# A recurrent layer's weights moved into tiles of their own, and all its loads moved to one queue

## The chip, the core and the metric

The kernel runs on one core of one Trainium2 chip. A core has a matrix engine (TensorE, "PE" in the profile), a vector engine (VectorE, "DVE"), an engine for functions and scaled copies (ScalarE, "ACT"), a general engine (GpSimd, "POOL") and an engine that mostly issues transfers (SyncE, "SP"). Each works through an instruction queue of its own, in order. SyncE and ScalarE issue the transfers (DMAs) here. Data lie in SBUF (128 partitions), results of matmuls in PSUM, inputs and outputs in the chip's main memory. The metric is the time of one execution on the device, in microseconds (us).

## The reference, cut to what matters

Four layers are applied one after the other to x (32 sequences of 64 tokens with 256 features), with a second input y of the same shape (ctx_2048 below).

```python
x = L0(x, y, ...)    # cross attention over channels, batches of 64 x 256
x = L1(x, y, ...)    # self attention, cross attention to y, MLP 256 -> 1024 -> 256
x = L2(x, y, ...)    # the same with other weights
x = L3(x, y, ...)    # recurrent layer, with state from y
```

The recurrent layer, L3, shortened:

```python
xn = _ln(x, ln1_w, ln1_b)
sx = _token_shift(xn, state[:, i1])
xxx = jnp.tanh((xn + sx * maa_x) @ maa_w1).reshape(b, l, 5, 1, EXTRA_MAA)
xxx = jnp.matmul(xxx, maa_w2).reshape(b, l, 5, E)
x5 = xn[:, :, None] + sx[:, :, None] * (maa_stack + xxx)
w = jnp.exp(-jnp.exp(time_decay + jnp.tanh(x5[:, :, 1] @ decay_w1) @ decay_w2))
r, k, v = x5[:, :, 3] @ Wr.T, x5[:, :, 0] @ Wk.T, x5[:, :, 2] @ Wv.T   # split in 32 heads of 8
g = silu(x5[:, :, 4] @ Wg.T)
# for each token: out = r (u * k v + s);  s = k v + w * s
att = group_norm(outs) * gn_w + gn_b
x = x + att * g @ Wo.T
xn2 = _ln(x, ln2_w, ln2_b); sx2 = _token_shift(xn2, state[:, i0])
xk, xr = xn2 + sx2 * ffn_maa_k, xn2 + sx2 * ffn_maa_r
x = x + sigmoid(xr @ ffn_Wr.T) * (square(relu(xk @ ffn_Wk.T)) @ ffn_Wv.T)
```

## The kernel before

The 2048 tokens are four groups (g = 0 to 3) of 512, and x stays in SBUF throughout. Layers 0, 1 and 2 go by groups, the MLPs by half groups of 256 tokens, the recurrent layer by eight slabs of 256 tokens (half a group each).

*Order.* Every layer is cut into pieces, small functions that emit a few instructions. `timed` spreads the pieces over a stretch of a made-up time axis, `emit` sorts all pieces by that time and runs them. On this axis layer 0 lies between -7.0 and -0.2 (L0_AT), the weights of layer 1's self attention at -4.0 (L0_LOAD), the MLP weights of layer 1 at 0.8 (MLP_LOAD), the self attention of L1 from 0 to 4, its cross attention from 4 to 8, and so on. The times are no times of the chip: they give each instruction a rank, and the tile framework then orders the queue of each engine by rank among the instructions which are ready by its own reckoning, so that a piece of a late rank with nothing to wait for can come early. It also adds the waits between engines. The transfers' completions are counted in eight counters in turn; a transfer waits for the one that was issued eight places before it, on whichever queue.

*Space.* Tiles come from pools. `const`, `small`, `psum`, `dram` and `work` are open all the time. `lw` and `lp` hold what the attention layers need, and are closed when these have been emitted. Then a pool `r` opens for the recurrent layer in the same place; with `reuse_waits="tile"` each of its tiles waits for the last users of the tiles of `lw` and `lp` that lay at its address, and all its instructions come behind the last instruction of these two pools in the order. The tag `big` in `work` is a ring of three buffers of 8 KB per partition, which the raw weights, the contexts ctxT, the MLP's hidden halves (hT) and the recurrent layer's products (vb) use in turn.

*The attention and MLP weights.* `staged` (L946) loads raw weights into `big` from SyncE, and ScalarE and VectorE split them into a high and a low part (`split_weights`, L956, L957; `split`, L178, L179; L1034, L1035).

*The recurrent pool* (L1081 to L1142). Eighteen tiles are loaded here: the W tiles (256 KB each) from SyncE, the small ones from ScalarE's queue, in the order of the code; `hold` only reserves places, so that each tile comes to lie where it does:

```python
def load(name, shape, src, eng=nc.scalar):
    c3[name] = pool.tile(shape, FP, name=name, bufs=1)
    eng.dma_start(c3[name], src)
```

*A slab* (`recurrent`). Its first part is: `norm` (statistics L146 to L152, x normalized on ScalarE at L155 into xn_r; TensorE transposes it, L163, and multiplies it with the matrix `step`, L170; ScalarE evacuates both, L625 and L632; GpSimd sets the first tokens from `st01`, L636), `first_mix` (L652), `maa` (products with mw1, L192 and L666, tanh at L671, a small rearranging transfer tb, L674), five times `mix` (product with mw2a or mw2b, L682, L686, L689), and the projections `vals` (Wv), `recept` (Wr), `keys` (Wk), `decay_a` and `decay_b` (dw1, dw2), `own_term` (selu, made from sel at L1137), `gate` (Wg). Its second part brings v through main memory into vb (`spread`, L722), multiplies it with k (L780), runs the scan (L795) and reads it with r (L780, pa at L808); norm, gate and Wo follow (L831, L841). Its third part is the feed-forward step (ffn_Wk, ffn_Wr, ffn_Wv) and the output (L884).

*Where the layers meet.* The last six half groups of L2's MLP (`late`: names L2m with pf, hf, hT, pfo) are put into the recurrent layer's plan, so that TensorE has work beside the slabs. L2's cross attention (names L2c) ends just before; its last output projection is po_L2c with the weights wo.

Of the kernel before, what the change touches and what calls it, by code (L numbers as in the profile page):

```python
# [15 lines left out]
FP = mybir.dt.float32  # L16
# [5 lines left out]
B, S, E = 32, 64, 256  # L22
T = B * S
P = 128
# [7 lines left out]
XM = 32  # L32
# [30 lines left out]
W3 = {n: i for i, n in enumerate(["Wk", "Wv", "Wr", "Wg", "Wo", "ffn_Wk", "ffn_Wr", "ffn_Wv"])}  # L63


def timed(pieces, t0, t1):

    total, at, out = sum(c for c, _ in pieces) or 1.0, 0.0, []
    for c, piece in pieces:
        out.append((t0 + (t1 - t0) * (at + c / 2) / total, piece))  # L70
        at += c
    return out


def emit(*timed_lists):
    for _, piece in sorted((p for ps in timed_lists for p in ps), key=lambda p: p[0]):
        piece()
# [3 lines left out]
def tile_xattn_stack(ctx: ExitStack, tc: tile.TileContext, a: dict, out: bass.AP):  # L81
    nc = tc.nc
    PSUM = bass.MemoryType.PSUM

    const = ctx.enter_context(tc.tile_pool(name="const", bufs=1))
# [31 lines left out]
    def row(name):  # L117

        r = const.tile([P, E], FP, tag="row", name=name, bufs=3)
        nc.scalar.dma_start(r, a["rows"][ROW[name]].partition_broadcast(P))  # L120
        return r
# [770 lines left out]
        return first, second, third  # L892


    wts = {}

    with tc.tile_pool(name="lw", bufs=1) as wp, tc.tile_pool(name="lp", bufs=2) as pool:
        m1 = wp.tile([P, S], FP, name="m1")
# [41 lines left out]
        def staged(name, k, parts):  # L940

            n = sum(n for _, n in parts)
            raw = work.tile([P, k, n], FP, tag="big", name=f"raw_{name}", bufs=3)
            at = 0
            for key, m in parts:
                nc.sync.dma_start(raw[:, :, at : at + m], a[key].rearrange("(c p) n -> p c n", p=P))  # L946
                at += m
            return raw

        def split_weights(w, raw, cols, scale=None, to=None):  # L950

            to = to or cols
            for c in range(raw.shape[1]):
                src, hi, lo = raw[:, c, cols], w[:, 0, c, to], w[:, 1, c, to]
                if scale:
                    nc.scalar.activation(hi, src, AF.Identity, bias=tiny[:, 2:3], scale=vec(scale, c))  # L956
                    nc.vector.scalar_tensor_tensor(lo, src, vec(scale, c), hi, ALU.mult, ALU.subtract)  # L957
                else:
                    split(hi, lo, src)
# [61 lines left out]
        def load_mlp(L):  # L1021
            def go():
                wts[L, "b2"] = row(f"{L}_b2")
                b = small.tile([P, 8], FP, tag="b1", name=f"b1_{L}", bufs=2)
                raw = staged(f"w1_{L}", 2, [(f"{L}_w1", FF)])
                ps = through(f"w1_{L}", raw, f"{L}_ln3_b", 8)
                nc.vector.tensor_tensor(b, vecs[:, VEC[f"{L}_b1"] : VEC[f"{L}_b1"] + 8], ps[:, :8], ALU.add)
                w1 = work.tile([P, 2, 2, FF], FPR, tag="w1", name=f"w1_{L}", bufs=1)
                split_weights(w1, raw, slice(0, FF), f"{L}_ln3_s")
                raw = staged(f"w2_{L}", 8, [(f"{L}_w2", E)])  # L1030
                w2 = work.tile([P, 2, 8, E], FPR, tag="w2", name=f"w2_{L}", bufs=1)
                for i in range(2):
                    cs = slice(4 * i, 4 * i + 4)
                    nc.scalar.copy(w2[:, 0, cs], raw[:, cs])  # L1034
                    nc.vector.tensor_tensor(w2[:, 1, cs], raw[:, cs], w2[:, 0, cs], ALU.subtract)  # L1035
                wts[L, "m"] = {"w1": w1, "w2": w2, "b1": b}
            return go
# [11 lines left out]
        plan = [timed(layer0(pool), *L0_AT), loads(load_self("L1"), L0_LOAD, L0_LOAD + 2.0)]  # L1049
        late = []  # L1050
        for i, L in enumerate(("L1", "L2")):
            for k in range(2):
                for g in range(NG):
                    a_ = (3 * i + k, f"{L}{'sc'[k]}", g, pool)
                    if k:
                        proj, core = attention(*a_, ctx_of(g), lambda L=L: wts[L, 2], mask_cross(g))
                    else:
                        proj, core = attention(*a_, None, lambda L=L: wts[L, 1], mask_self)
                    at = (8 + GAP) * i + 4 * k + g
                    p0 = at + PROJ + (CPROJ if k else 0)  # L1060
                    if g == 0 and (i or k):
                        plan.append(loads((load_cross if k else load_self)(L), p0 - 0.9, p0 - 0.001))
                    plan += [timed(proj, p0, p0 + PROJ_D), timed(core, at, at + CORE_D)]
            at = (8 + GAP) * i + MLP
            for g in range(NG):
                for u in range(2):
                    p = mlp_half(3 * i + 2, f"{L}m{g}{u}", g, u, lambda L=L: wts[L, "m"], lambda L=L: wts[L, "b2"])
                    if i and g:

                        s = (2 * g + u - 2) * SLOT + M2  # L1070
                        late += timed(p, s, s + M2_D)
                        continue
                    plan.append(timed(p, at, at + MLP_D))
                    at += MLP_S
            load = at - MLP_S + MLP_D + 0.001 if i == 0 else None
            plan.append([(load, load_mlp("L2"))] if i == 0 else [(MLP_LOAD, load_mlp("L1"))])
        emit(*plan)

    with tc.tile_pool(name="r", bufs=2, reuse_waits="tile") as pool:  # L1081
        c3 = {}

        def load(name, shape, src, eng=nc.scalar):
            c3[name] = pool.tile(shape, FP, name=name, bufs=1)
            eng.dma_start(c3[name], src)

        def load_w(*names):
            for n in names:
                load(n, [P, 2, E], a["w3"][W3[n]].rearrange("(c p) n -> p c n", p=P), nc.sync)  # L1090

        def hold(tag, bufs=2, shape=None):
            pool.tile(shape or [P, 2, RR], FP, tag=tag, name=f"hold_{tag}", bufs=bufs)

        def shifted_ring(name):

            c3[name] = ring(pool, name, [P, 2, RB, S], 2, lambda t: nc.gpsimd.memset(t[:, :, :, 0], 0.0))

        load("mw1", [P, 2, 5 * XM], a["maa_w1"].rearrange("(c p) n -> p c n", p=P))
        load("mw2a", [P, E], a["maa_w2"][:P])  # L1100
        load("mw2b", [XM, E], a["maa_w2"][P:])
        load("step", [P, P], a["step"])
        load("st01", [P, 2, B, 2], a["st01"])
        load("dw1", [P, 2, 64], a["decay_w1"].rearrange("(c p) n -> p c n", p=P))
        hold("fx")
        hold("dfx")
        load("avg", [P, P], a["avg"])
        hold("x5", 3)
        hold("nx", 1)
        shifted_ring("wsh")  # L1110
        hold("xk")
        hold("xr")
        hold("kk")
        hold("x")
        hold("rr", 2, [P, 2, E])
        hold("dx")
        load_w("Wv", "Wr", "Wk")
        shifted_ring("vsh")

        load("sel", [P, 2, P], a["sel"])  # L1120
        load("dw2", [64, E], a["decay_w2"])
        hold("ta", 1, [P, RR + S])
        hold("vT")
        hold("rT")
        hold("tb", 1, [XM, RR])
        hold("rk", 1)
        hold("dT", 1, [64, RR])
        selu = c3["selu"] = pool.tile([P, 2, P], FP, name="selu", bufs=1)
        load_w("Wg", "Wo", "ffn_Wk", "ffn_Wr", "ffn_Wv")
        load("s0", [P, 2, RS, B], a["s0"])  # L1130
        hold("gt")
        hold("at")
        hold("sq", 1)
        shifted_ring("ksh")
        hold("nfx", 1)
        for c in range(2):
            nc.vector.tensor_scalar(selu[:, c], c3["sel"][:, c], vec("L3_faaaa", c), None, ALU.mult)  # L1137
        gnh = c3["gnh"] = pool.tile([P, 4], FP, name="gnh", bufs=1)
        for i, n in enumerate(("L3_gn_w", "L3_gn_b")):
            nc.vector.tensor_scalar(  # L1140
                gnh[:, 2 * i : 2 * i + 2], vecs[:, VEC[n] : VEC[n] + 2], 0.5, None, ALU.mult
            )  # L1142
        r = [recurrent(n, pool, c3) for n in range(2 * NG)]
        plan = []
        for n, (first, second, third) in enumerate(r):
            at = n * SLOT + START
            plan += [timed(first[:1], at - LEAD, at - LEAD), timed(first[1:], at, at + R1_D)]
            at += R2
            plan += [timed(second, at, at + R2_D)]
            at += R2_D + F0  # L1150
            plan += [timed(third[:1], at, at), timed(third[1:], at + F1, at + F1 + F1_D)]
        plan.append(late)
        emit(*plan)
# [78 lines left out]
```

## Time and profile before

| | before |
|---|---|
| median of 3 runs | 1092.89 us (1092.37 to 1093.71) |
| profiled execution | 1097.71 us |
| its span | 1095.9 us |
| mean granted TensorE clock | 0.958 |
| TensorE busy | 985.5 us |
| VectorE busy | 813.4 us |
| ScalarE busy | 551.0 us |
| GpSimd busy | 532.2 us |
| share of 16 DMA engines: SyncE's queue (q1) | 16.5%, 48.55 MB |
| share of 16 DMA engines: ScalarE's queue (q10) | 1.2%, 3.16 MB |

The stages of the profiled execution: layer 0 and the first loads up to about 104 us, layers 1 and 2 to about 706 us, recurrent layer with the last MLP halves to the end.

How to read it. The profile is of one execution; the medians are of others, without a profile. Busy time of TensorE is the modelled time of its matmuls. A group "out<-in" names the tile that is written and those that are read. "SPq" and "ACTq" are the issues of transfers from SyncE's and ScalarE's queues; their duration is that of the issue and not of the transfer. A wait "A <- B: 5.8, 1, 5.8" says that A waited 5.8 us in all for B, once, 5.8 us at most. The chain of waits goes back from the last instruction to what released it each time, so that its pieces add up to the span.

### The profile page before, as it was taken

To read this page: it belongs to the slowest core of one execution; us is meant where nothing else is said; L and a number is where in the kernel's file an instruction comes from. 1 tells how busy PE (TensorE), PEld (TensorE's weight loads), DVE (VectorE), ACT (ScalarE), POOL (GpSimd) and SP (SyncE) were. 2 spreads that over 40 slices of the span, in tenths; PEclk is the share of its full clock that TensorE was granted. 3 is DMA by queue.
4 is the path that set the end of the run, shared out by engine and by line. 5 is a ranking of instruction groups with operands and counts; after the bars stand their busy time and mean duration, and the time that the engine had idled before them with its cause. 6 is when DMAs were issued, how large, how long until landed. Compare 5 with 4: busy or idle time off the path is not lost.

```text
span 1095.9 us, 26331 instructions
## 1 busy us (share of the span) xinstructions
PE 985.5 (90%) x10764; PEld 789.9 (72%) x10764; DVE 813.4 (74%) x1513; ACT 551.0 (50%) x1271; POOL 532.2 (49%) x552
## 2 busy tenths in 40 slices
PE   8998999899989999989989999898889989869757
PEld 5777776667778989867767778786767777647535
DVE  5754687878877545687778777549798897988873
ACT  5643653555555645754555454354446554345234
POOL 4243766767756435566557756342534523233300
PEclk9899998999999999988999999999999999989788
DMA  9100111111100000141011101222222122430300
GB/s 300 42 21 20 20 47 31 39 24 26 29 16 20 27 1 21 50 130 41 21 41 27 26 22 31 59 79 50 61 66 50 41 59 56 121 87 21 87 10 29
DMA packets 45947, 53.39 MB, mean 49 GB/s; under 512 B 16146, under 2 KB 40068, under 8 KB 43780
## 3 DMA queue, kind: packets, MB, share of 16 engines
q1 hardware_dynamic: 38756, 48.55, 16.5%
q10 hardware_dynamic: 7072, 3.16, 1.2%
q8 instruction: 85, 1.39, 0.5%
q14 instruction: 34, 0.28, 0.1%
HBM read 38.83 MB, written 4.21 MB: 39 GB/s over the span
## 4 chain that ended last, share of the span: by engine, by line
PE 41%; DVE 35%; POOL 8%; ACT 7%; DMA 4%; issue 4%; SPq 1%; ACTq 0%; POOLq 0%; DVEq 0%
DVE vb_r L795 6%; DVE vb_r L780 4%; PE pf_L1m L187 4%; PE pfo_L1m L187 3%; POOL s_L2c L463 2%; PE pfo_L2m L187 2%; DVE x L198 2%; PE pr L312 2%; POOL s_L1c L463 2%; PE pf_L2m L187 2%; DVE x_r L686 1%; PE pq_L2c L187 1%; PE px_r L682 1%; DVE s_L1c L458 1%; POOL s_L1s L463 1%
## 5 line engine op out<-in xcount | busy, mean ns | idle before, releaser
L689 POOL TENSOR_TENSOR x_r<-x_r,xn_r 128x512 f32<-128x512 f32 x40 | 58.2, 1463 | 93.2 <-DVE x_r L686 91.0
L795 DVE TENSOR_TENSOR_SCAN vb_r<-wsh,vb_r 128x512 f32<-128x512 f32 x64 | 76.4, 1250 | 5.9 <-ACT wsh L693 5.9
L187 PE MATMUL pf_L2m<-lnT_L2m,w_L 128*128 128x256 f32 x384 | 57.0, 302 | 6.5 <-DVE lnT_L2m L179 3.7
L463 POOL TENSOR_TENSOR s_L1s<-s_L1s,n 128x512 f32<-128x512 f32 x32 | 43.1, 1358 | 39.8 <-DVE s_L1s L458 39.1
L187 PEld LDWEIGHTS pf_L2m<-lnT_L2m,w_L 128*128 128x128 f32 x384 | 51.1, 200 | 10.7 <-DVE lnT_L2m L179 4.3
L187 PE MATMUL pfo_L2m<-w_L,hT_L2m 128*128 128x256 f32 x384 | 55.4, 293 | 1.6 <-DVE hT_L2m L581 1.5
L463 POOL TENSOR_TENSOR s_L2s<-s_L2s,n 128x512 f32<-128x512 f32 x32 | 43.1, 1365 | 27.0 <-DVE s_L2s L458 26.3
L187 PE MATMUL pfo_L1m<-w_L,hT_L1m 128*128 128x256 f32 x384 | 54.5, 288 | 1.6 <-POOL hT_L1m L580 0.8
L463 POOL TENSOR_TENSOR s_L2c<-s_L2c,n_L2c 128x512 f32<-128x512 f32 x32 | 41.7, 1322 | 29.2 <-DVE s_L2c L458 28.2
L187 PE MATMUL pf_L1m<-lnT_L1m,w_L 128*128 128x256 f32 x384 | 52.0, 288 | 3.9 <-ACT hf_L1m L577 1.2
L463 POOL TENSOR_TENSOR s_L1c<-s_L1c,n_L1c 128x512 f32<-128x512 f32 x32 | 41.3, 1308 | 24.3 <-DVE s_L1c L458 23.2
L187 PEld LDWEIGHTS pf_L1m<-lnT_L1m,w_L 128*128 128x128 f32 x384 | 47.5, 191 | 7.2 <-ACT hf_L1m L577 2.1
L187 PEld LDWEIGHTS pfo_L2m<-w_L,hT_L2m 128*128 128x128 f32 x384 | 49.3, 192 | 4.8 <-DVE hT_L2m L581 1.9
L187 PEld LDWEIGHTS pfo_L1m<-w_L,hT_L1m 128*128 128x128 f32 x384 | 49.2, 191 | 3.5 <-POOL hT_L1m L580 1.0
L580 POOL TENSOR_SCALAR hT_L1m<-hf_L1m 128x512 fp32r<-128x512 f32 x32 | 21.9, 684 | 55.4 <-ACT hf_L1m L577 53.5
L132 PE MATMUL pa_r<-vb_r,sel 128*32 128x256 f32 x256 | 23.2, 494 | 27.7 <-DVE vb_r L780 25.3
L577 ACT ACTIVATE hf_L1m<-pf_L1m,b_L 128x256 f32<-128x256 f32 x64 | 26.7, 472 | 42.3 <-PE pf_L1m L187 39.7
L581 DVE TENSOR_TENSOR hT_L1m<-hf_L1m,hT_L1m 128x512 fp32r<-128x512 f32 x32 | 25.3, 791 | 30.2 <-POOL hT_L1m L580 30.1
L580 POOL TENSOR_SCALAR hT_L2m<-hf_L2m 128x512 fp32r<-128x512 f32 x32 | 26.7, 840 | 42.7 <-ACT hf_L2m L577 42.6
L577 ACT ACTIVATE hf_L2m<-pf_L2m,b_L 128x256 f32<-128x256 f32 x64 | 26.6, 472 | 36.4 <-PE pf_L2m L187 29.4
L780 DVE TENSOR_TENSOR vb_r<-vb_r,ksh 128x2048 f32<-128x2048 f32 x16 | 40.1, 2523 | 4.4 <-DMA vb_r<-vd_r 4.4
L282 ACT ACTIVATE att<-pe,nmx 128x256 f32<-128x256 f32 x64 | 29.6, 478 | 20.2 <-DVE nmx L280 17.6
(388 smaller groups left out, 3073.3 us busy)
## 6 DMA issues: line engine op xcount, KB each, us to landing
vb_r<-vd_r SPq DMA_DIRECT2D x16, 1024.0 KB, 7.1
raw_w_L<-in_L_w_dram SPq DMA_DIRECT2D x4, 1024.0 KB, 12.4
y<-in_y_dram SPq DMA_DIRECT2D x8, 256.0 KB, 5.3
x<-in_x_dram SPq DMA_DIRECT2D x8, 256.0 KB, 4.8
ctxT_L1c<-in_yT_dram SPq DMA_DIRECT2D x4, 512.0 KB, 3.7
kbd<-kT_L1s SPq DMA_DIRECT2D x64, 32.0 KB, 2.0
kbd<-kT_L1c SPq DMA_DIRECT2D x64, 32.0 KB, 2.0
kbd<-kT_L2s SPq DMA_DIRECT2D x64, 32.0 KB, 2.2
```

Of the source, the lines that this page charges most:

```text
L132: return lambda: nc.tensor.matmul(ps, sta, mov, start=start, stop=stop)
L187: nc.tensor.matmul(ps, sta[x], mov[y], start=(at == 0), stop=(at == n - 1))
L198: nc.vector.tensor_tensor(xs, xs, ps, ALU.add)
L282: nc.scalar.activation(att[:, 2 * h + c, :], pe[:, c, :], AF.Exp, bias=nmx[:, h, c : c + 1], accum_out=rs[:, h, c : c + 1],)
L312: nc.tensor.matmul(pr[:, m, h, :], att[:, 2 * h + c, m * P : (m + 1) * P], xvT[:, c, h, :], start=(c == 0), stop=(c == 1),)
L463: nc.gpsimd.tensor_tensor(s[:, r], s[:, r], n(j).unsqueeze(1).broadcast_to([P, 8, S]), ALU.add)
L577: nc.scalar.activation(raw[:, i], ps[:, i], AF.Gelu_apprx_tanh, bias=w()["b1"][:, 2 * f2 + i : 2 * f2 + i + 1])
L580: nc.gpsimd.tensor_scalar(h[:, 0], raw, 1.0, 0.0, ALU.mult, ALU.add)
L581: nc.vector.tensor_tensor(h[:, 1], raw, h[:, 0], ALU.subtract)
L689: nc.gpsimd.tensor_tensor(d, d, st["x"], ALU.add)
L780: nc.vector.tensor_tensor(v, v, x.unsqueeze(1).broadcast_to([P, 4, 2 * RR]), ALU.mult)
L795: nc.vector.tensor_tensor_scan(v[:, d], flat(st["wsh"]), v[:, d], 0.0, ALU.mult, ALU.add)
```

## The change

A function `load_early` is put into the plan of the attention layers, at 4.0, the start of layer 1's cross attention. It loads twelve tiles (step, mw1, st01, mw2a, mw2b, Wv, Wr, Wk, dw1, dw2, sel, avg) from SyncE's queue into the pool `const`, where they have places of their own to the end. The remaining six loads of the recurrent pool (Wg, Wo, ffn_Wk, ffn_Wr, ffn_Wv, s0) stay where they were in the program and all go to SyncE's queue; s0 was on ScalarE's. So the recurrent pool holds less, and its tiles move to lower addresses. To make room, the framework's scratch for software-issued DMAs is given 1024 bytes per partition; in the kernel before it had 16,384.

```diff
-    wts = {}
+    wts, c3 = {}, {}
+
+    def load_to(pool, name, shape, src):
+        c3[name] = pool.tile(shape, FP, name=name, bufs=1)
+        nc.sync.dma_start(c3[name], src)
+
+    def load_early():
+
+        load_to(const, "step", [P, P], a["step"])
+        load_to(const, "mw1", [P, 2, 5 * XM], a["maa_w1"].rearrange("(c p) n -> p c n", p=P))
+        load_to(const, "st01", [P, 2, B, 2], a["st01"])
+        load_to(const, "mw2a", [P, E], a["maa_w2"][:P])
+        load_to(const, "mw2b", [XM, E], a["maa_w2"][P:])
+        for n in ("Wv", "Wr", "Wk"):
+            load_to(const, n, [P, 2, E], a["w3"][W3[n]].rearrange("(c p) n -> p c n", p=P))
+        load_to(const, "dw1", [P, 2, 64], a["decay_w1"].rearrange("(c p) n -> p c n", p=P))
+        load_to(const, "dw2", [64, E], a["decay_w2"])
+
+        load_to(const, "sel", [P, 2, P], a["sel"])
+        load_to(const, "avg", [P, P], a["avg"])
...
+        plan.append([(4.0, load_early)])
         emit(*plan)
...
-        c3 = {}
-
-        def load(name, shape, src, eng=nc.scalar):
-            c3[name] = pool.tile(shape, FP, name=name, bufs=1)
-            eng.dma_start(c3[name], src)
+        def load(name, shape, src):
+            load_to(pool, name, shape, src)
 
         def load_w(*names):
             for n in names:
-                load(n, [P, 2, E], a["w3"][W3[n]].rearrange("(c p) n -> p c n", p=P), nc.sync)
+                load(n, [P, 2, E], a["w3"][W3[n]].rearrange("(c p) n -> p c n", p=P))
...
-        load("mw1", ...), load("mw2a", ...), load("mw2b", ...), load("step", ...), load("st01", ...), load("dw1", ...)
         hold("fx")
         hold("dfx")
-        load("avg", [P, P], a["avg"])
...
-        load_w("Wv", "Wr", "Wk")
         shifted_ring("vsh")
-
-        load("sel", [P, 2, P], a["sel"])
-        load("dw2", [64, E], a["decay_w2"])
...
-    nc = bacc.Bacc("TRN2", target_bir_lowering=False, num_devices=1)
+    nc = bacc.Bacc("TRN2", target_bir_lowering=False, num_devices=1, dynamic_dma_scratch_size=1024)
```

## The prediction

> **What bounds the kernel now.** I read the page first, then the chain of waits in order of time, then the waits of the stretch where the chain rests on DMAs, then the busy time by window around it.
>
> ```profile
> PE 985.5 (90%) x10764; PEld 789.9 (72%) x10764; DVE 813.4 (74%) x1513; ACT 551.0 (50%) x1271; POOL 532.2 (49%) x552
> ...
> PE 41%; DVE 35%; POOL 8%; ACT 7%; DMA 4%; issue 4%; SPq 1%; ACTq 0%; POOLq 0%; DVEq 0%
> ```
>
> TensorE is busy for 90% of the span, and 41% of the chain that ended last is TensorE, 35% VectorE; DMA is 4%. Loading weights is therefore nothing in general and can only matter in a few places. The largest of them lies where the attention layers end and the recurrent layer begins:
>
> ```profile
> 704.12 1.64 PE pf_L2m L187 x12
> ...
> 705.78 0.84 ACT hf_L2m L577 x2
> ...
> 706.73 2.32 DMA mw2b<-in_maa_w_dram
> ...
> 709.07 3.35 DMA avg<-in_avg_dram
> ...
> 712.45 0.61 ACT xn_r L155
> ...
> 713.10 0.33 PE pln_r L163
> ```
>
> For 2.32 + 3.35 = 5.67 us the chain consists of loads (mw2b, avg), with a matmul before and the recurrent layer's first normalization (xn_r, L155) after. The waits of 703 to 732 us, and the windows, say who pays:
>
> ```profile
> DVE selu L1137 <- DMA sel<-in_sel_dram: 6.3, 1, 6.3
> ACT xn_r L155 <- DMA avg<-in_avg_dram: 5.8, 1, 5.8
> ```
>
> ```profile
> 706.00:708.00 2.00, 1.54 (x13) 1.34 (x13) 1.75 (x4) 0.62 (x2) 0.62 (x1) 1.00 0.53 148
> 708.00:710.00 2.00, 2.00 (x19) 2.00 (x18) 0.06 (x1) 0.00 (x0) 0.00 (x0) 1.00 0.63 128
> 710.00:712.00 2.00, 0.52 (x5) 0.32 (x3) 0.00 (x0) 0.00 (x0) 0.00 (x0) 1.00 1.10 337
> 712.00:714.00 2.00, 0.90 (x7) 0.77 (x8) 0.00 (x0) 1.55 (x4) 0.00 (x0) 1.00 0.91 307
> 714.00:716.00 2.00, 2.00 (x14) 2.00 (x13) 1.64 (x3) 2.00 (x6) 1.26 (x2) 0.64 0.39 129
> 716.00:718.00 2.00, 2.00 (x12) 2.00 (x11) 1.70 (x4) 2.00 (x5) 0.22 (x1) 0.51 0.00 0
> 718.00:720.00 2.00, 2.00 (x18) 1.61 (x17) 0.73 (x2) 1.50 (x4) 1.04 (x2) 1.00 0.03 8
> ```
>
> (Columns: busy PE, PEld, DVE, ACT, POOL, then the granted clock, DMA share, GB/s.) ScalarE stands still for 5.83 us because ten load issues lie in its queue in front of xn_r, and in the compiled program a DMA waits for the one issued eight places before it, so the later ones wait for the earlier ones to land. The MLP's GELUs (L577) queue behind them, so TensorE runs out too: 0.46 us idle in 706 to 708, 1.48 in 710 to 712, 1.10 in 712 to 714, 3.04 in all. Then it works at a granted clock of about 0.5 until 718.
>
> **The change, part by part.**
>
> *Ten loads leave ScalarE's queue.* Nine go to SyncE's early loads, s0 to SyncE's late ones. Their issue rows in the timeline are 0.37 + 0.48 + 0.44 + 0.43 + 0.44 + 0.39 + 0.39 + 0.44 + 0.49 + 0.54 = 4.41 us, and the rest of the 5.83 is waiting for landings. xn_r has its statistics since 701.04 (nmr_r), so it follows hf_L2m, which ends at 706.62, instead of starting at 712.45: 5.83 us earlier on ScalarE. What is late next is TensorE: its 24 pf_L2m matmuls run from 706.68 to 709.81 anyway, and transposes, pf_L2m and pfo_L2m follow without the hole. So the gain lies between TensorE's 3.04 us of idle time (it alone binds) and ScalarE's 5.83 us (the whole stall binds). Between them lies the slow clock: 12 pf_L2m matmuls took 1.64 us at clock 1.00 (704.12) and 2.56 us at 714.93, which is 0.92 us; 12 pfo_L2m took 1.69 us at 717.50 against half of 3.07 us for the 24 at 720.41, which is 0.16 us. I take TensorE's own account, 3.04 + 0.92 + 0.16 = 4.1 us, because TensorE is the busiest engine and the chain is on it before and after.
>
> The clock row is 0.64 and 0.51 right behind a hole of 2.58 us (710.52 to 713.10), so I count its 1.1 us as part of the hole. The Trainium skill ("TensorE: Matmul & The Clock Gate", Why this matters for your kernels) says that gaps of up to some 3 us leave the clock up; by that rule the slow clock would have another cause and stay, and the gain would be 3.0 us. The trace differs here: the clock was halved behind 2.58 us.
>
> *Twelve loads in front of other work in SyncE's queue.* load_early stands at time 4.0 in the plan, behind the MLP weights of L1 (MLP_LOAD 0.8). Its tiles are new, with nothing to wait for, and the program is ordered by when things are ready: the mask of a cross attention's second group, planned at 4.1, is issued at 8 us. So I expect the twelve right behind raw_w1 and raw_w2, in layer 0:
>
> ```profile
> 16.53 1.10 SPq L946 DMA_DIRECT2D raw_w_L<-in_L_w_dram  x2
> 34.01 0.37 SPq L946 DMA_DIRECT2D raw_L<-in_L_w_q_dram  x1
> ```
>
> ```profile
> 7.96 0.95 ACTq L910 DMA_DIRECT2D m_L1c<-in_m_dram  x2
> ...
> 29.64 1.99 ACT L1034 CAST w_L<-raw_w_L 128x1024 fp32r<-128x1024 f32 x2 [1.69 <-DMA raw_w_L<-in_L_w_dram]
> ```
>
> SyncE is free from 17.63 to 34.01. Twelve issues at about 0.43 us (rows of 0.37 to 0.49) are 5.2 us. Wk is the eighth, waits for raw_w2 to land at 29.64, and four more follow by 31.4; behind them wait raw_L (34.01, which needs VectorE until 33.98), then ctxT at 58.9 and the first kbd copy at 94.6. Cover left: 2.6 us. The bytes are 1536 KB (768 of W, 160 + 128 + 32 of mw, 128 sel, five times 64). At the 354 to 397 GB/s of 18 to 26 us that is 4.2 us. The engines are full until about 27 us and at 0.04 to 0.02 share from 28 to 34. If the bytes stay behind raw_w1 and raw_w2 they cost nothing; if they get ahead, the ScalarE wait at 29.64 (1.69 us today) grows by up to 4.2 us. A gain is excluded, since nothing in layer 0 loses a wait. I take 0, because these loads are issued after the two on the same queue, and the DMA rows behind 28 us are empty.
>
> *Space.* The held tiles add 13,568 bytes per partition, the scratch shrinks by 15,360, and the recurrent pool's remaining tiles slide down over others: sx_r now over layer 2's last wo, whose last reader po_L2c ends at 706.22; x5 over vbd, last read until 700.86. Both are free before the earliest new use (sx_r about 709.5), so no term. The page lists no software DMA queue, so the smaller scratch costs nothing.
>
> *Six loads left behind* (Wg, Wo, three ffn, s0), all on SyncE: their places are free once L2c's last score transposes end (698.8), their first uses are s at 745.79 and Wg at 755.33, and the next SyncE work, tb_r, is at 720.94 (some 6 us earlier in the new order). Zero, with over 10 us of cover; without it, 6 x 0.43 = 2.6 us.
>
> *What carries to the end.* From 750 to 1050 us TensorE is busy 40 to 47 and VectorE 42 to 45 of every 50 us, so I let the shift carry whole. Its bounds are those of the rivals below: given back entirely, or overpaid by 7.7 us.
>
> Sum: the profiled execution took 1097.71 us (span 1095.9), 0.44% above the median of 1092.89. 1097.71 - 4.1 = 1093.6; scaled by 1092.89 / 1097.71, 1088.8 us. By the bounds, 1089.9 (3.0) to 1087.1 (5.8).
>
> **Rivals.**
>
> *Slower: the ring of three "big" buffers.* The late MLP's hT (two for each half) and the slab's vb (two) share it. If slab 0, now early, takes a buffer before L2m's next half, that half stalls, or the other way round; all later slabs inherit the order. For it: SyncE's fetches of vb wait 80.6 us in 6 waits for other vb (longest 19.5) and 27.1 us in 4 for pfo_L2m; and the chain has one bare fetch of 7.67 us (836.20). Against it: the plan's order of the pieces is unchanged. Price: one more bare fetch, -4.1 + 7.7 = +3.6, so 1096.5. It decides once the order of spread and hidden on the ring differs from today's. 0.24.
>
> *Given back.* VectorE is only 1.62 of 5 us busy from 735 to 740, before the first long multiply at 741.76, so slab 0 may wait for something else there, and the 4.1 us return: 1092.9. Against it: TensorE has no hole there (5.00 of 5). 0.15.
>
> *Bytes ahead of raw_w2 in layer 0:* +4.2 - 4.1, so 1093.0. The Trainium skill ("DMA: Bandwidth & Descriptors", Queues, rings and completion order) says that on each DMA engine one queue's descriptors are consumed in ring order, which would rule this out; no run here shows it. 0.05.
>
> *The loads really go in layer 1,* at their planned time, in front of kbd copies which the scores wait for: +5.2 - 4.1, so 1094.0. The mask at 7.96 us speaks against it. 0.03.
>
> *More than the sum:* the new order on the ring covers that bare fetch too, -4.1 - 7.7 at most, so 1081.1 at the far end. Nothing in the order favours it over the slower case but the earlier start of slab 0. 0.08.
>
> **How the numbers follow.** The forecast, 1088.8, has 0.45. About 0.2% (2.2 us) is what a measurement of this kernel can tell from no change. Faster: 0.45 + 0.08 = 0.53. Within: 0.15 + 0.05 + 0.03 = 0.23. Slower: 0.24. Signs are mixed, so the forecast's own range is 1087.1 to 1089.9, and the range for 8 in 10 goes from 1083.5 (most of the way to the far end of the larger gain) to 1097.5 (just past the ring's price).
>
> **What would show it.** Right: none of the recurrent layer's loads in ScalarE's queue, SyncE issuing the twelve between 17 and 32 us, xn_r right behind hf_L2m, no TensorE hole and no half clock in the stretch that answers to 710 to 718, stretches before it unmoved, and everything behind some 4 us earlier. Wrong: a ScalarE wait above 1.69 us for raw_w2; kbd copies of L1c held up; or the same start gained and lost again by a longer vb wait between there and the end.

## The result and the profile after

The changed kernel has a median of 1091.01 us (22 runs), the kernel before 1093.76 us in the same comparison (22 runs): ratio 0.9974, 95% interval 0.9963 to 0.9985, that is 2.75 us less (1.6 to 4.0). A second comparison, told below, gave 0.9954 (0.9937 to 0.9972). The forecast was a ratio of 0.9963 (1088.8 / 1092.89). It lies on the lower end of the first interval and inside the second. The profiled execution after took 1089.03 us, its span 1087.2 us, its mean granted clock 0.963.

From the page of the changed kernel, busy times and shares of the chain that ended last:

```profile
PE 982.4 (90%) x10764; PEld 787.1 (72%) x10764; DVE 814.3 (75%) x1513; ACT 550.4 (51%) x1271; POOL 531.4 (49%) x552
...
PE 40%; DVE 33%; POOL 8%; ACT 6%; DMA 5%; issue 4%; SPq 2%; ACTq 0%; POOLq 0%; DVEq 0%
```

TensorE's busy time is 3.1 us less, the other engines' all but the same. The chain of waits, in order of time, at the place where the recurrent layer begins:

```profile
700.16 1.61 PE pf_L2m L187 x12
701.80 0.85 ACT hf_L2m L577 x2
702.69 2.90 PE pf_L2m L187 x22
705.59 0.11 PE pln_r L163
705.70 0.22 PE pst_r L170 x2
```

The two DMA pieces (mw2b, avg) of 5.67 us are gone. pln_r, which was at 713.10, 8.98 us behind the first pf_L2m (704.12), is now at 705.59, 5.43 us behind it (700.16), and only TensorE's own pf_L2m stands between. ScalarE's timeline shows why:

```profile
701.80 0.84 ACT L577 ACTIVATE hf_L2m<-pf_L2m,b_L 128x256 f32<-128x256 f32 x2 [0.89 <-PE pf_L2m L187]
702.53 1.09 ACT L155 ACTIVATE xn_r<-x,nmr_r,rstd_r 128x256 f32<-128x256 f32 x2
```

xn_r (L155) follows hf_L2m at once. Busy time by window (PE, PEld, DVE, ACT, POOL, then granted clock, DMA share, GB/s), at the same distances from the first pf_L2m as 708 to 716 us of before:

```profile
704.16:706.16 2.00, 2.00 (x19) 2.00 (x19) 0.30 (x2) 0.84 (x2) 0.62 (x1) 1.00 0.00 0
706.16:708.16 2.00, 2.00 (x19) 2.00 (x18) 0.59 (x1) 1.75 (x4) 0.00 (x0) 1.00 0.00 0
708.16:710.16 2.00, 2.00 (x18) 1.97 (x17) 0.98 (x3) 2.00 (x6) 1.10 (x2) 1.00 0.00 0
710.16:712.16 2.00, 2.00 (x28) 1.55 (x26) 1.25 (x2) 1.98 (x5) 0.80 (x2) 1.00 0.03 8
```

No hole, no half clock, and DMA only in the last row. (The short hole of 0.46 us, which before lies in 706 to 708 us, has its like just ahead of these rows: TensorE is idle from 702.23 to 702.69.) And SyncE's timeline in layer 0:

```profile
16.59 1.12 SPq L965 DMA_DIRECT2D raw_w_L<-in_L_w_dram  x2
19.30 2.43 SPq L899 DMA_DIRECT2D step<-in_step_dram  x1
...
25.62 0.38 SPq L899 DMA_DIRECT2D Wr<-in_w_dram  x1
28.59 0.37 SPq L899 DMA_DIRECT2D Wk<-in_w_dram  x1
...
30.75 0.43 SPq L899 DMA_DIRECT2D avg<-in_avg_dram  x1
34.07 0.38 SPq L965 DMA_DIRECT2D raw_L<-in_L_w_q_dram  x1
```

The twelve early loads (L899) go out between 19.30 and 31.18, right behind raw_w1 and raw_w2, Wk waits as expected, and the next transfer, raw_L, is issued at 34.07, against 34.01 before. The first of them took 2.43 us to issue, and the twelve took 7.9 us together, not 5.2; SyncE had the room for it.

A ruler for all that follows: the stretch from the chain's first pf_L2m to the first pk_r of slab 0, two events of TensorE that every version has in the same order. The window lines of before and after:

```profile
704.12:738.39 34.27, 31.05 (x223) 27.43 (x224) 15.01 (x35) 16.12 (x35) 12.62 (x17) 0.95 0.37 101
```

```profile
700.16:729.28 29.12, 28.66 (x224) 25.86 (x224) 14.46 (x36) 16.11 (x35) 12.94 (x21) 1.00 0.19 47
```

34.27 us became 29.12 us: 5.15 us less, of which TensorE's idle time gives 2.76 (34.27 - 31.05 = 3.22 before, 29.12 - 28.66 = 0.46 after) and its busy time 2.39.

### The profile page after: what moved, and what is told of

Same layout as the page of the kernel before. It is cut to its first block, busy times and chain, and to the rows that moved or that the text cites. A ratio compares the mean times of both kernels' runs of the same rounds, so it can differ in the third digit from the quotient of the medians.

```text
span 1087.2 us, 26321 instructions
## 1 busy us (share of the span) xinstructions
PE 982.4 (90%) x10764; PEld 787.1 (72%) x10764; DVE 814.3 (75%) x1513; ACT 550.4 (51%) x1271; POOL 531.4 (49%) x552
## 4 chain that ended last, share of the span: by engine, by line
PE 40%; DVE 33%; POOL 8%; ACT 6%; DMA 5%; issue 4%; SPq 2%; ACTq 0%; POOLq 0%; DVEq 0%
DVE vb_r L795 6%; DVE vb_r L780 4%; PE pf_L1m L187 4%; PE pfo_L1m L187 3%; PE pf_L2m L187 3%; POOL s_L2c L463 2%; PE pfo_L2m L187 2%; DVE x L198 2%; POOL s_L1c L463 2%; SPq L403 2%; DMA raw_w_L<-in_L_w_dram 2%; PE pr L312 1%; PE px_r L682 1%; DVE s_L1c L458 1%; PE pwo_r L841 1%
## 5 line engine op out<-in xcount | busy, mean ns | idle before, releaser
L149 POOL TENSOR_SCALAR rstd_fr<-mv_fr 128x2 f32<-128x2 f32 x8 | 6.1, 763 | 66.1 <-DVE mv_fr L147 56.2
```

## The experiments

Theory A: the cost was the ten issues in ScalarE's queue ahead of xn_r, and nothing else in the change earns or costs. Rival B: the weights had to be there early, which only holding them gives. A second question was where the difference lies between 5.15 us at the transition and 2.75 us between the medians.

**The old order a second time, and the new one.** The kernel before with the small DMA scratch alone:

```diff
-    nc = bacc.Bacc("TRN2", target_bir_lowering=False, num_devices=1)
+    nc = bacc.Bacc("TRN2", target_bir_lowering=False, num_devices=1, dynamic_dma_scratch_size=1024)
```

> The kernel before, with the DMA scratch of the change (1024 bytes) and nothing else. Every theory of mine says no difference: ratio 0.999 to 1.001. Its profile is a second one of the old order: ScalarE's stall in front of xn_r again 5 to 6 us and TensorE's hole again 2 to 3 us; the half clock behind that hole again at 714 to 718 us if the hole causes it, and elsewhere if it only fell there.

> The changed kernel once more, for a second profile and the same rounds as the others. Ratio to before 0.996 to 0.9985 (it was 0.9974). If the stretches of half granted clock outside the transition stand at other places than in the first profile of the changed kernel (10 to 13, 35 to 42 us of the one or other), the 3.8 us by which the changed kernel was ahead at 46 us and the 1 to 9 us by which its lead swung later are the clock's and not the change's. If they stand at the same places, the order of the early loads moves the clock and is part of the result.

Measured: 0.9996 (0.9975 to 1.0018) for the scratch alone, so no part of the gain shows in it; 0.9954 (0.9937 to 0.9972) for the changed kernel, a little under what I expected (0.996 to 0.9985). The windows of the ruler, old order (with the small scratch) and new order:

```profile
701.32:735.23 33.91, 31.10 (x223) 27.48 (x224) 14.81 (x36) 16.27 (x35) 12.60 (x17) 0.95 0.36 102
```

```profile
704.58:733.71 29.13, 28.67 (x224) 25.86 (x224) 14.46 (x36) 16.13 (x35) 12.95 (x21) 1.00 0.19 47
```

33.91 against 29.13 us: 4.78 us, with 5.15 in the first pair. The new order repeats to 0.01 us. From the first hf_L2m of the transition to the end of the span the old order took 1088.8 - 702.97 = 385.8 us and the new one 1086.9 - 706.21 = 380.7 us, 5.1 us less: in this pair, what is gained at the transition is still there at the end. What differs between executions lies elsewhere. The new order's second profile was 3.3 us *later* than the old one's when the transition began (704.58 against 701.32), although the two are the same program up to there but for the early loads. Those are not it: at 50 us the new order was 0.8 us ahead; it lost 2.7 us between 190 and 240 us and 1.6 about 620 us, both times near a place where a stretch of half clock fell at another place (210 against 205 us) or was missing in the other (623 to 626). Half the clock was granted at 10 to 13 us in the first profile of the changed kernel and at 36 to 39 in the second; at 754 to 757 and 798 to 808 in the first, at 763 to 766 and 801 to 804 in the second. Of the 8.7 us between the first two spans, 3.96 were there when the transition began (704.12 against 700.16), 5.15 are the ruler's, and 0.4 were lost again behind it (357.5 us from the first pk_r to the end before, 357.9 after). That the 3.96 us come from where the half clock fell is likely and was not tested: at 50 us, the three profiles of this document with half clock at 10 us and not at 35 (changed kernel, ten issues, nineteen issues) were 1.7 to 2.5 us ahead of the changed kernel's second profile, and the three others with it at 35 and not at 10 whose layer 0 has nothing in its way (before, small scratch, five issues) were 0.8 to 1.8 us behind it.

**All loads from SyncE, at their old places.** The kernel before with one word changed:

```diff
-        def load(name, shape, src, eng=nc.scalar):
+        def load(name, shape, src, eng=nc.sync):
```

> The kernel before, with every load of the recurrent layer issued by SyncE instead of ten of them by ScalarE, each at its old place in the order; nothing is loaded early, no tile is held. Theory A (the ten issues in ScalarE's queue are the cost): xn_r comes right behind hf_L2m, TensorE has no hole of 1.5 us or more between pf_L2m and pln_r, and the time is as low as the changed kernel's, ratio to before 0.995 to 0.9985. Rival B (the weights have to be there early): the loads now land later behind SyncE's other issues, a DMA row (mw2b, avg or Wv) is back in the chain between 700 and 735 us with 2 us or more, and the ratio is 0.999 or above.

Measured: 0.9952 (0.9933 to 0.9970), as low as the changed kernel in the same comparison (0.9954). Its window, and SyncE's timeline:

```profile
702.30:731.74 29.44, 28.95 (x223) 25.86 (x224) 14.29 (x36) 16.35 (x35) 12.60 (x17) 1.00 0.42 122
```

```profile
657.59 0.43 SPq L1086 DMA_DIRECT2D dw<-in_decay_w_dram  x1
699.10 0.33 SPq L1086 DMA_DIRECT2D avg<-in_avg_dram  x1
699.48 0.44 SPq L1086 DMA_DIRECT2D Wv<-in_w_dram  x1
...
705.58 0.41 SPq L1086 DMA_DIRECT2D s<-in_s_dram  x1
714.64 2.47 SPq L674 DMA_DIRECT2D tb_r<-ta_r  x4
```

SyncE issues avg, Wv and ten more only between 699.10 and 705.99, beside the very matmuls in question (DMA share 0.42 over the window), and the stretch is 29.44 us all the same. The first six (mw1, mw2a, mw2b, step, st01, dw1) go out from 655.23 to 658.02, where ScalarE had issued them from 705.79 on, so these six are early here too, though not held from layer 0. What falls of rival B is the holding: places from layer 0 on, with 13,568 bytes of space per partition and the shrunken scratch, are worth 0.3 us on the ruler and nothing that the times show. The change of queue alone is worth the rest. Whether the six would have cost something by coming late, this run doesn't say; the next one has all weights early and the issues back.

**The issues back, the weights still early.** The changed kernel, with ten issues put back into ScalarE's queue:

```diff
+        def again(name, shape, src):
+            t = pool.tile(shape, FP, name=f"again_{name}", bufs=1)
+            nc.scalar.dma_start(t, src)
+
+        again("mw1", [P, 2, 5 * XM], a["maa_w1"].rearrange("(c p) n -> p c n", p=P))
...
-        load("s0", [P, 2, RS, B], a["s0"])
+        c3["s0"] = pool.tile([P, 2, RS, B], FP, name="s0", bufs=1)
+        nc.scalar.dma_start(c3["s0"], a["s0"])
```

> The changed kernel, with ten issues put back into ScalarE's queue at their old places: nine load the same data once more into spare tiles that nobody reads, the tenth is s0's own; the early loads stay as they are. Theory A (issues cost): ScalarE stands still for 4.4 to 5.8 us in front of xn_r, TensorE's hole of some 2.5 us is back, xn_r starts 4.4 to 5.8 us later than in the changed kernel against hf_L2m's end, and the ratio to the kernel before is 0.999 to 1.002. Rival B (data that come late cost, and here they are there early): ratio 0.995 to 0.9985 as in the changed kernel, ScalarE's stall under 2 us or hidden.

Measured: 0.9992 (0.9969 to 1.0014), so no gain is left that the interval tells from zero, although every weight is there. Its waits at the transition and its window:

```profile
ACT xn_r L155 <- DMA again_dw<-in_decay_w_dram: 4.2, 1, 4.2
```

```profile
699.24:731.29 32.05, 30.14 (x223) 25.99 (x224) 14.18 (x36) 16.01 (x35) 13.22 (x19) 1.00 0.32 83
```

The DMA that the wait is put down to (a spare copy of dw) was needed by nobody; the ten issues themselves stand back to back from 700.89 to 705.86, the first 0.8 us of them beside hf_L2m, and are the 4.2 us. The stretch is 32.05 us, 2.93 longer than the changed kernel's, which is 2.93 of the 5.15 us between old and new order: the issues alone are more than half of it on the ruler, and the rest came with the waits for landings and the half clock, which this version doesn't have. Stall and hole were smaller than I expected (4.4 to 5.8 us, some 2.5 us): 4.2 us, and 0.95 us of TensorE's idle time in front of pln_r. The clock stayed at 1.00 behind the smaller hole, and yet TensorE's busy time is 1.48 us higher than after (30.14 against 28.66). Why the same matmuls are busy for longer at the same clock is left open.

**Five issues, and nineteen.** The same edit with the first five loads only, and with each spare load issued twice:

```diff
             nc.scalar.dma_start(t, src)
+            u = pool.tile(shape, FP, name=f"more_{name}", bufs=1)
+            nc.scalar.dma_start(u, src)
```

> The changed kernel, with only the first five of the ten issues put back into ScalarE's queue (the same data loaded once more into spare tiles that nobody reads); fewer than eight, so none waits for an earlier one to land. ScalarE stands still for 2.0 to 2.3 us in front of xn_r. From ten issues (stall of 4.2 us, stretch from the chain's first pf_L2m to pk_r of slab 0 longer by 2.9 us than the changed kernel's 29.1) the cover would be 1.3 us: theory A, the stretch is 29.8 to 30.3 us and the time 0.5 to 1.2 us above the changed kernel's. Rival B (TensorE's 24 pf_L2m matmuls of 2.9 us cover the whole of such a stall): 29.0 to 29.4 us.

> The changed kernel, with nineteen issues in ScalarE's queue in front of xn_r (the nine spare loads of the run with ten issues, each issued twice, and s0's). 19 issues of 0.45 us are 8.5 us, with waits for earlier loads to land 8.5 to 12 us of stall. Theory A (the stall costs what goes beyond a cover of 1.3 us, and carries to the end): the stretch from the chain's first pf_L2m to pk_r of slab 0 is 36 to 40 us and the ratio to the kernel before 1.002 to 1.006. Rival B (delays at the transition are taken up later by slack in the recurrent layer): the stretch as long, but the ratio 0.998 to 1.001.

Measured: 0.9964 (0.9943 to 0.9985) with five, 1.0033 (1.0008 to 1.0058) with nineteen. ScalarE's wait and the window of each, five first:

```profile
ACT xn_r L155 <- DMA again_mw2a<-in_maa_w_dram: 1.5, 1, 1.5
```

```profile
702.40:731.77 29.37, 28.78 (x223) 25.91 (x224) 14.46 (x36) 16.13 (x35) 13.23 (x19) 1.00 0.30 80
```

```profile
ACT xn_r L155 <- DMA more_sel<-in_sel_dram: 9.3, 1, 9.3
```

```profile
702.13:740.39 38.26, 31.62 (x223) 28.31 (x224) 14.18 (x36) 16.34 (x35) 13.04 (x17) 0.91 0.34 90
```

The stall with the stretch, in us:

| | ScalarE's stall | stretch | above the changed kernel | 29.12 + (stall - 1.26) |
|---|---|---|---|---|
| changed kernel | 0 | 29.12 | 0 | |
| five issues | 1.5 | 29.37 | 0.25 | 29.4 |
| ten issues | 4.2 | 32.05 | 2.93 | 32.1 |
| before, small scratch | 5.4 | 33.91 | 4.79 | 33.3 |
| before | 5.8 | 34.27 | 5.15 | 33.7 |
| nineteen issues | 9.3 | 38.26 | 9.14 | 37.2 |

The 1.26 is fitted: it is the stall of ten issues, 4.19 us, less the 2.93 that they cost, so that row lies on the line by construction. Read this way, the first 1.26 us of the stall are covered by TensorE's pf_L2m matmuls, and every further one costs a microsecond; the row of five issues lies on the line too. The three rows in which half the clock was granted behind the hole (clock 0.95, 0.95, 0.91 over the window) lie 0.6 to 1.1 us above that line. With five issues theory A's number missed: I had expected a stall of 2.0 to 2.3 us, and it was 1.5, because the first two issues run beside hf_L2m. It fits the line, but it fits the rival as well (29.0 to 29.4 us). The nineteen cost the kernel about what the ruler says: 1.0033 less 0.9954 is 0.0079, or 8.6 us, against 9.1; the two intervals leave some 3 us either way.

**The early loads from another engine, and in another place.** In the changed kernel, the twelve early loads issued by ScalarE; and, in another version, issued by SyncE ahead of raw_w1 and raw_w2 (planned just ahead of MLP_LOAD):

```diff
-        nc.sync.dma_start(c3[name], src)
+        (nc.scalar if pool is const else nc.sync).dma_start(c3[name], src)
```

```diff
-        plan.append([(4.0, load_early)])
+            if i:
+                plan.append([(MLP_LOAD - 0.001, load_early)])
```

> The changed kernel, with its twelve early loads issued by ScalarE instead of SyncE, in layer 0; the six late ones stay with SyncE. Theory A (an issue costs the time of the engine that issues it, wherever that engine is waited for): twelve issues of 0.4 to 0.5 us are 4.8 to 6 us of ScalarE's time between 8 and 30 us; layer 0 ends 2 to 6 us later than in the changed kernel and the ratio to the kernel before is 0.998 to 1.001, while the transition stays as short as in the changed kernel (29.1 us from the chain's first pf_L2m to pk_r of slab 0). Rival B (layer 0 has slack on ScalarE, so only the place at the transition was dear): ratio 0.995 to 0.9975 as the changed kernel.

> The changed kernel, with its twelve early loads issued by SyncE ahead of raw_w1 and raw_w2 of L1 instead of behind them. The disputed price of 4.2 us for bytes that get ahead: theory A, ScalarE's wait for raw_w2 (1.7 us at about 29.6 us) grows to 4 to 8 us, the end of layer 0 moves by 2 to 5 us and the ratio to the kernel before is 0.998 to 1.001. Rival B (the order of the program gives way, since the weights of L1's MLP are needed only much later): the wait grows but nothing behind 60 us moves by more than the 1 to 3 us by which two executions differ, ratio 0.995 to 0.9975.

Measured: 0.9995 (0.9974 to 1.0015) from ScalarE, 1.0011 (0.9995 to 1.0027) ahead of the raw weights; theory A both times, by the ratio. From ScalarE the gain is lost although the transition is as short as ever:

```profile
705.77:734.93 29.16, 28.70 (x224) 25.89 (x224) 14.47 (x36) 16.13 (x35) 12.94 (x21) 1.00 0.19 47
```

It is lost in layer 0: the first scores of layer 1 (s_L1s on VectorE) start at 107.1 us, against 101.1 and 103.6 in the changed kernel's two profiles. There raw_w1 and raw_w2 go out later too (21.09 us instead of 16.59), and what of the delay is ScalarE's issues and what the later loads, the run doesn't separate. Ahead of the raw weights, SyncE's timeline and ScalarE's, then the windows of all engines:

```profile
16.84 0.39 SPq L899 DMA_DIRECT2D step<-in_step_dram  x1
...
26.54 0.43 SPq L899 DMA_DIRECT2D avg<-in_avg_dram  x1
27.01 0.94 SPq L965 DMA_DIRECT2D raw_w_L<-in_L_w_dram  x2
```

```profile
32.62 2.37 ACT L975 ACTIVATE w_L<-raw_w_L,tiny,vecs 128x1024 fp32r<-128x1024 f32 x2 [2.70 <-DMA raw_w_L<-in_L_w_dram]
...
48.15 0.69 ACT L336 ACTIVATE r<-pt,vecs 128x512 f32<-128x512 f32 x1 [8.39 <-PE pt L331]
```

```profile
40.00:50.00 10.00, 9.56 (x42) 7.77 (x43) 3.84 (x12) 0.69 (x1) 3.40 (x5) 0.55 0.33 107
```

raw_w1 and raw_w2 go out at 27.01 instead of 16.59, ScalarE's cast of the first (w_L) waits 2.70 us for it with layer 0's attention queued behind (I expected 4 to 8), and then half clock is granted from 35 to 49 us, so that ScalarE waits 8.39 us more for TensorE (pt) and works 0.69 us of the ten from 40 to 50. At 690 us this kernel is 5.8 us behind the changed kernel's second profile. What of it is the wait and what the slow clock that came with it, the run doesn't separate; the 4.2 us which the prediction put on bytes that get ahead are of the order of the whole loss, and not of the wait that it named; and it was the place in SyncE's queue that kept them at 0.

**The holes and the clock.** The ten profiles so far allow a count. From 5 us on TensorE has 277 idle holes of 1.0 us or more in them; in the table, how many of these had a stretch of half clock begin in the hole or up to 5 us behind it.

| length of hole, us | holes | followed by half clock |
|---|---|---|
| 1.0 to 1.5 | 147 | 51 |
| 1.5 to 2.0 | 44 | 26 |
| 2.0 to 2.5 | 28 | 19 |
| 2.5 and more | 58 | 57 |

145 of the 158 stretches of half clock begin so; by chance alone, with 16 such stretches per 1090 us and some 6.5 us that count behind each hole, one hole in ten would be followed.

The length of a hole is not what decides, though. Within one profile all stretches of half clock begin whole multiples of 3.413 us apart, to 0.001 us. If the span is cut along this grid, the share of a window in which TensorE is busy tells whether half clock begins with the next window. Of the windows at full clock in the ten profiles:

| TensorE busy in the window | windows | half clock in the next |
|---|---|---|
| under 40% | 74 | 74 |
| 40 to 70% | 244 | 77 |
| over 70% | 2604 | 2 |

So a hole counts by how much of one window it empties: a short one is followed by half clock or not by how it lies to the grid and by what else is idle in the same window. In the hole of the transition the windows ahead of the half clock were 43% busy before (711.14 to 714.56) and 37% with the small scratch; with ten issues back no window there was under 72%, and the clock stayed at 1.00.

The longest holes stand in front of the readout pa_r in the last three slabs. I filled them in the changed kernel with spare matmuls, 38 of them and, in a second version, half as many:

```diff
+    FILL = {5: 12, 6: 10, 7: 16}
...
                 st["pa"] = both(f"pa_{t}", "pd")
+                for _ in range(FILL.get(n, 0)):
+                    nc.tensor.matmul(
+                        flat2(st["pa"]), st["wsh"][:, 0, 0:2].rearrange("p b t -> p (b t)"), flat2(c3["Wv"]),
+                        start=True, stop=True,
+                    )
```

> The changed kernel, with 38 spare matmuls of 128x512 (results never read) in slabs 5, 6 and 7 (12, 10 and 16), traced in front of the readout pa_r, where TensorE has its longest holes (6.9 to 7.6, 6.2 and 8.9 to 9.2 us, each followed by 7 to 14 us at half the clock in every profile so far). Theory C (the half clock comes from the holes and costs time behind them): the holes are down to 1 to 4 us, half clock behind 960 us falls from some 38 us to 5 to 25 us, and the end comes 2 to 8 us earlier, ratio to the kernel before 0.989 to 0.994. Rival D (the half clock falls where it will, whatever TensorE does, or the spare matmuls delay as much as they save): ratio 0.995 to 1.000, with the half clock behind 960 us still 30 us or more or the same chain length.

> As the run with the holes filled, with half as many spare matmuls (6, 5 and 8). By theory C holes of 2.5 us and more are followed by the half clock in 57 of 58 cases in the profiles so far, those of 1.0 to 1.5 us in 51 of 147; half filled, the three holes stay at 3 to 6 us in all, so most of the half clock stays and the gain is 0 to 4 us below the changed kernel: ratio 0.992 to 0.997. Rival D: as the changed kernel, 0.995 to 0.998.

Measured: 0.9982 (0.9966 to 0.9999) filled, 0.9950 (0.9932 to 0.9968) half filled. The windows of 1000 to 1050 us, changed kernel (second profile), half filled, filled:

```profile
1000.00:1050.00 50.00, 33.80 (x186) 24.01 (x184) 47.55 (x60) 18.21 (x37) 11.57 (x8) 0.86 0.23 58
```

```profile
1000.00:1050.00 50.00, 44.93 (x224) 29.18 (x224) 47.33 (x56) 16.82 (x33) 7.91 (x8) 0.98 0.24 58
```

```profile
1000.00:1050.00 50.00, 50.00 (x212) 32.01 (x213) 45.32 (x57) 17.16 (x35) 8.48 (x8) 1.00 0.23 58
```

The clock follows the holes: 0.86, then 0.98 with TensorE at 44.93 of 50 us, then 1.00 with no idle time at all. Half clock between 960 us and the end fell from 30 us to 11 and to 2 us, in the half-filled version too, where I had expected most of it to stay. But the time does not follow the clock: theory C's 0.989 to 0.994 for the filled version missed, and rival D had the time right. A spare matmul (which the profile counts as two) took 0.86 us and not the 0.43 that I had counted with, so half filled (6.9 us in the hole of 9) was the dose that I had meant, and filled was twice that; TensorE was then all but never idle, and the readout had to queue behind it (the last slab's starts at 1053.68 us, against 1045.90 half filled). Half filled, the ratio, 0.9950, is that of the changed kernel: VectorE is busy for 45 to 48 of the 50 us in every version, and the slower clock of TensorE lay beside that. Theory C is right about the cause of the half clock and wrong about its price against this profile. That no slow clock there ever costs time is not shown: the changed kernel's first profile, with a clock of 0.80 in the same window, lost 3.3 us against its second between about 1000 and 1050 us, and whether the clock made it so was not tested. No version here beats the changed kernel by more than the intervals.

## Why the prediction was right

*Ten loads out of ScalarE's queue.* Shown from both sides: taking them out alone gives all of the gain (0.9952), and the same ten issues put back cost 2.93 of the 5.15 us on the ruler, with every weight early (0.9992). The place (xn_r right behind hf_L2m), the engine (TensorE's idle time) and the bounds (3.0 to 5.8) held: 5.15 and 4.78 us on the ruler. The 5.83 us of stall were 4.2 for the issues alone and 1.6 for waiting for earlier loads to land. The prediction's split, 4.41 and 1.42, is close partly by luck: some 0.8 us of its 4.41 lie ahead of the stall, beside hf_L2m, and it left out the short gaps between two issues.

*The terms that were mis-sized.* The forecast was 3.04 us of idle time and 1.08 of slow clock; the ruler has 2.76 of idle time and 2.39 of busy time. Of the idle time, the first hole of 0.46 us was counted as gained, and it is still there in the new order (702.23 to 702.69). Of the busy time, I compared 12 pf_L2m at half clock (2.56 us) with 12 that were themselves waiting for their input (1.64); in the new order 12 take 1.43, so that term is 1.13 and not 0.92. With the forecast's 0.16 for pfo_L2m this makes 1.29 us; the remaining 1.10 had no term in the sum. The run with ten issues has busy time of this size, 1.48 us, at full clock, so it needn't come from the slow clock; what it is stays open. One error was too large and two too small, so it is in part luck that 4.1 lies between the two differences of medians, 2.75 and 5.0 us.

*The clock rule.* By the Trainium skill ("TensorE: Matmul & The Clock Gate", Why this matters for your kernels) the half clock behind a hole of 2.58 us would have had another cause and stayed. Here the measurement decides against the rule: the half clock stood behind the hole in both profiles of the old order (holes of 2.6 and 2.2 us), it was gone with the hole in both profiles of the changed kernel and in the one with all loads from SyncE, and holes of 1.0 to 2.5 us were followed by it in 96 of 219 cases. By the table of windows it is the busy share of a window of 3.413 us that decides, and a hole of 2.2 us, well placed, is enough.

*Twelve loads in front of other work.* As forecast: 19.30 to 31.18, next issue at 34.07, no cost to be seen; with a place ahead of the raw weights the kernel was 5.8 us late at 690 us, against a bound of 4.2. The Trainium skill's ring order ("DMA: Bandwidth & Descriptors", Queues, rings and completion order) is not contradicted: issued behind raw_w1 and raw_w2, the early bytes held up neither. ScalarE waited 0.8 and 1.6 us for the raw weights in the two profiles of the changed kernel, and 1.7 and 2.0 us in those of the old order; the order of the bytes itself no run shows.

*Space, late loads.* The scratch alone gave 0.9996. The late six went out between 660.25 and 687.58 from SyncE, earlier than the 698.8 from which I had thought their places free, and nobody waited for them.

*What carries to the end.* All of it, where profiles can be compared. From the first pk_r of slab 0, the end of the ruler, to the end of the span, the ten profiles ahead of the spare matmuls fall into two kinds, and both hold profiles of the old order and of the new. In one, with a stretch of 13.7 us of half clock that begins between 1013 and 1022 us, it takes 356.4 to 359.0 us: 357.5 before, 357.9 in the changed kernel's first profile. In the other, where that stretch begins between 1041 and 1051 us, it takes 353.2 to 354.6: 353.6 in the old order with the small scratch, 353.2 in the changed kernel's second profile, 354.6 with nineteen issues. So within the spread of a kind (2.6 and 1.4 us) neither the 5 us between the orders nor the 9 us of nineteen issues are given back. The medians don't say it as clearly: the first interval (1.6 to 4.0 us) ends just short of the 4.1, and four comparisons of versions without the long stall give 0.9974, 0.9952, 0.9954 and 0.9964. Why the first is the highest is left open. Should the executions without a profile be of the same two kinds, some 4 us apart, a median would move with their mix; that is argued and not tested.

*Rivals.* The ring of three "big" buffers didn't flip: the compiled orders of before and after differ only around the transition (706 to 733 us) and by the moved loads, and the bare fetch of vb is there as before, with 7.27 us at 829.92 (7.67 at 836.20). Nothing was given back behind the transition, and the loads went out in layer 0, not in layer 1.

## What to carry to other kernels

A transfer's issue is work of the engine that issues it, 0.4 to 0.5 us each at the transition here (one took 2.43 us on SyncE in layer 0), and its price is read from what is queued behind it: ten in front of a normalization that TensorE waits for cost 3 us with nobody waiting for their data, twelve on an idle queue cost nothing, the same twelve on ScalarE in layer 0 cost some 4, the later loads behind them included. Before weights are held early, try the one-word change that moves the issue to an idle engine; here it earned everything that the times show. A ruler between two events around the edit repeated to 0.4 us or better, where the medians had intervals of 2 us either way.

## What was not expected of the hardware

The granted clock fell behind holes much shorter than I would have thought: 35% of the holes of 1.0 to 1.5 us, 98% of those of 2.5 us or more. What decided was the busy share of a window of 3.413 us on a fixed grid: under 40% half clock always followed (74 of 74), over 70% all but never (2 of 2604). Stretches of half clock came at different places in executions of one program, and the profiles differ by 1 to 3 us about such places; the times of the kernel before ran from 1089.25 to 1097.24 us in the first comparison. And a higher clock was worth nothing in a stretch where VectorE was busy for 47 of 50 us: 0.86 or 0.98, same time.
